# Layer 0 attention: unpadded transposes of eight heads at a time, and the second batch's keys, squares and powers half a step earlier

## The chip, the core and the metric

The kernel runs as one program on one core of a Trainium2 chip. A core has five engines that each work through their own queue of instructions in order: TensorE (PE; its weight loads are listed as PEld), VectorE (DVE), ScalarE (ACT), GpSimd (POOL) and SyncE (SP, which issues most DMAs). TensorE writes its results to PSUM, and DVE or ACT has to move them from there to SBUF, an "eviction". The metric is the device time of one execution in microseconds; the median of three runs stands for a kernel.

## The reference

The reference is four layers, each of a cross attention and a feed-forward part, over x of shape 4 x 256 x 256 and a context of 4 x 512 x 128. Only the attention of layer 0 is touched:

```python
# x: (4, 256, 256), y: the context (4, 512, 128); H = 16 heads of HD = 16, DCA = 16
def _ln(t, w, b):
    m = jnp.mean(t, axis=-1, keepdims=True)
    v = jnp.var(t, axis=-1, keepdims=True)
    return (t - m) * jax.lax.rsqrt(v + EPS) * w + b
y_dca = y[:, -DCA:, :]
y_main = y[:, :-DCA, :]
kv_dca = (y_dca @ Wkv_dca + bkv_dca).reshape(b, DCA, 2, H, HD)
k_dca = _ln(kv_dca[:, :, 0], kn_dca_w, kn_dca_b)
v_dca = kv_dca[:, :, 1]
q = _ln((x @ Wq + bq).reshape(b, s1, H, HD), qn_w, qn_b)
kv = jnp.concatenate([y_main @ Wk + bk, y_main @ Wv + bv], axis=-1)
kv = kv.reshape(b, s2, H, 2 * HD)
k = _ln(kv[..., :HD], kn_w, kn_b)
v = kv[..., HD:]
# softmax attention of q over (k, v), and another of q over (k_dca, v_dca); per head
ctx = ctx + ctx_dca
return ctx @ Wo + bo
```

What comes in is a layer norm of x, and the result is added to x. Queries and keys are normalised head by head: every group of 16 numbers gets its mean taken off and is divided by its own deviation, and then gets a weight and a bias, which are the same for all heads.

## The kernel before

**Stages.** All matrix work is in 32-bit floats. Layer 0's attention is the first stage of the program, some 150 of its 1,423 us; `bounded_path` holds it, and the order of its instructions is that of the text, on each engine. Four batches (b = 0 to 3) of 256 queries and 512 keys go through it, with two query chunks (NC) and four key chunks (NK) of 128 tokens, NQK = 6 in all. The last key chunk holds 112 ordinary keys (RD) and the 16 separate ones.

**How a batch is prepared.** `layernorm_T` transposes the normalised x, `project_q` and `project_k` compute raw queries and keys into the tile `qk` (tokens on the partitions, 16 heads x 16 numbers along a row); each returns the DVE addition that evicts it. The class `Scale` then divides by the deviation: `square` (ACT for batch 0, POOL for the others), `sum` on DVE, `power` (two small ACT instructions), `product` on DVE, which writes the tile `pad`. In `pad` each head has 32 columns, of which 16 are zeros from a memset at the start, so four heads fill 128 columns. `transposed` turns `pad` by chunks: four transposes of 128 x 128 for a chunk, into one PSUM bank `pT`, and from there an eviction to `qT` or `kT` that multiplies with the weight and adds the bias per partition (`cols`). Even chunks are evicted by ACT, odd ones by DVE; the last chunk takes two evictions, since its 16 separate keys have other weights. `norm_columns` makes `cols` at the start, by one-column matmuls from the row `rep`.

**How a batch is computed.** For each group of four heads (hg = 0 to 3) there are two half steps (kp = 0, 1), which cover two key chunks each; i = 2 hg + kp counts the eight half steps of a batch. In each, `scores` issues eight matmuls (16 passes) that contract over the 16 rows of a head, with four heads side by side at rows 0, 32, 64 and 96, into four PSUM banks `ps`, and four exponentials on ACT. `values` issues the products of the group before with the values. `quotient`, after the second half, divides on DVE. Between them, two functions issue the preparation of the next batch n = b + 1: `ahead`, between scores and values, and `between`, after the values.

| half step i | before: work for batch n |
|---|---|
| 0 | transposes of the norm (and of the context for n > 1) |
| 1 | queries |
| 2 | keys, square |
| 3 | values (n > 1), sum |
| 4 | power |
| 5 | product (ahead), the statistics of batch n + 1 (between) |
| 6 | transposes of chunks 0 to 2, tokens of batch n + 1 |
| 7 | transposes of chunks 3 to 5 (ahead) |

**What sets the order around the change.** Each engine takes its instructions in the order written. All PSUM tiles of this stage except the outputs (`o`, two banks) come from a ring of six: tile number k waits until all that read tile k - 6 are done. Four of the six are taken by each half step's scores. The tiles `qk`, `hs` (the squares) and `pad` exist once; `kT` and `qT` twice.

The lines that are used below: L1092 (memset of the pad), L1105 (memset of rep), L1175 (queries), L1191 and L1193 (keys), L1205 (values' projection), L1229 (square on POOL), L1232 (sum), L1237 and L1238 (power), L1242 to L1245 (product), L1255 (columns), L1316 (transposes), L1328 (evictions on DVE), L1330 (evictions on ACT), L1341 (scores), L1345 (exponentials), L1351 and L1360 (values), L1374 to L1382 (quotient), L918 to L921 (statistics), L926 (tokens), L938 (transposes of the norm).

Of the kernel before, what the change touches and what calls it, by code (L numbers as in the profile page):

```python
# [9 lines left out]
F32 = mybir.dt.float32  # L10
# [826 lines left out]
def bounded_path(ctx: ExitStack, tc: tile.TileContext, t, out: bass.AP, over):  # L837
# [189 lines left out]
    with tc.manual_schedule(engines={E.PE, E.Activation, E.DVE, E.Pool}):  # L1027
# [20 lines left out]
        takes = rows1[:, D:].rearrange("n (i p) -> n i p", p=P)  # L1048


        brow = w0.tile([1, 2, 2 * D], F32, tag="kT", name="brow")
        rep = w0.tile([1, 6, 4, 32], F32, tag="qT0", name="rep")
        prm = l0.tile([1, 3, 2, HD0], F32, tag="prm", name="prm")
        nc.sync.dma_start(crow[0:1, 0, :], t["L0_bq"].partition_broadcast(1))
        for i, n in enumerate(("L0_bkv", "L0_bdca")):
# [12 lines left out]
            load_x(b)  # L1068

        wo0 = l0.tile([P, 2, D], F32, tag="wo0", name="wo0")  # L1070
        wo0r = t["L0_wo"].rearrange("(q o j i x) n -> o j i x q n", q=2, o=2, j=4, i=2)
        for o in range(2):
            for j in range(4):
                r0 = 32 * j + HD0 * (1 - o)
# [13 lines left out]
        nc.gpsimd.memset(neghalf, -0.5)  # L1088


        pad = l0.tile([P, NQK * H0, 32], F32, tag="pad", name="pad")
        nc.vector.memset(pad[:, :, HD0:], 0.0)  # L1092

        nc.gpsimd.memset(takes, 1.0)
        for i, base, cm, p in (
# [70 lines left out]
        def last_context(b):  # L1166
            nc.gpsimd.tensor_copy(c_last[:, b % 2, 0, :RD], cT[:, b, SK - P : SKM])
            nc.gpsimd.tensor_copy(c_last[:, b % 2, 1, RD:], cT[:, b, SKM:])

        def project_q(b):  # L1170
            qks[b] = w0.tile([P, NQK, D], F32, tag="qk", name=f"qk{b}", bufs=1)
            pq = bank("mm", [P, NC, D], f"pq0_{b}")
            for c in range(NC):
                for d in range(ND):
                    nc.tensor.matmul(  # L1175
                        pq[:, c, :],
                        lhsT=xnTs[b][:, d, c * P : (c + 1) * P],
                        rhs=wq0[:, d, :],
                        start=(d == 0),
                        stop=(d == ND - 1),  # L1180
                    )
            return lambda: nc.vector.tensor_tensor(
                qks[b][:, :NC, :], pq, bqk[:, 0:1, :].to_broadcast([P, NC, D]), ALU.add
            )

        def project_k(b, k0):
            pk = bank("mm", [P, 2, D], f"pk{b}_{k0}")
            for k in (k0, k0 + 1):
                last = k == NK - 1
                ck = c_last[:, b % 2, 0, :] if last else cT[:, b, k * P : (k + 1) * P]  # L1190
                nc.tensor.matmul(pk[:, k - k0, :], lhsT=ck, rhs=wk0[:, 0, :], start=True, stop=not last)  # L1191
                if last:
                    nc.tensor.matmul(  # L1193
                        pk[:, k - k0, :], lhsT=c_last[:, b % 2, 1, :], rhs=wk0[:, 1, :], start=False, stop=True
                    )
            bias = bqk[:, 1:3, :] if k0 + 2 == NK else bqk[:, 1:2, :].to_broadcast([P, 2, D])
            return lambda: nc.vector.tensor_tensor(qks[b][:, NC + k0 : NC + k0 + 2, :], pk, bias, ALU.add)
# [14 lines left out]
        class Scale:  # L1212


            def __init__(self, b, a, z):
                self.n, self.name = z - a, f"{b}_{a}"
                self.src = by_head(qks[b][:, a:z])
                self.dst = pad.rearrange("p (c h) x -> p c h x", h=H0)[:, a:z, :, :HD0]
# [28 lines left out]
                )  # L1247


        cols = l0.tile([P, 3, 2], F32, tag="cols", name="cols")  # L1250

        def norm_columns():
            pn = bank("o", [P, 6], "pcols")
            for i in range(6):
                nc.tensor.matmul(  # L1255
                    pn[:, i : i + 1],
                    lhsT=rep[:, i].rearrange("o h x -> o (h x)"),
                    rhs=ident[:1, :1],
                    start=True,
                    stop=True,  # L1260
                )
            c_v = cols.rearrange("p i a -> p (i a)")
            nc.vector.tensor_scalar(c_v[:, :2], pn[:, :2], HD0 ** -0.5, None, ALU.mult)
            nc.vector.tensor_copy(c_v[:, 2:], pn[:, 2:])

        def score_bound():

# [13 lines left out]
        def bias_rows():  # L1281

            b5 = [
                brow[:, i, :].rearrange("a (q o j i x) -> a q o j i x", q=2, o=2, j=4, i=2)[:, :, :, :, 1] for i in range(2)
            ]
            for o in range(2):
                nc.vector.tensor_tensor(bval[:, :, :, 1 - o], b5[0][:, :, o], b5[1][:, :, o], ALU.add)
# [15 lines left out]

        kTs, qTs = {}, {}

        def transposed(b, chunks):

            if b not in kTs:
                kTs[b] = w0.tile([P, 4, SK], F32, tag="kT", name=f"kT{b}")
                qTs[b] = w0.tile([P, 4, S], F32, tag="qT0", name=f"qT0_{b}")  # L1310
            kT, qT = kTs[b], qTs[b]
            for c in chunks:
                pt = bank("t", [P, 4, P], f"pT{b}_{c}")
                for hg in range(4):
                    r0 = c * H0 + 4 * hg
                    nc.tensor.transpose(  # L1316
                        pt[:, hg, :], pad[:, r0 : r0 + 4, :].rearrange("p h x -> p (h x)"), ident
                    )
                if c < NC:
                    parts = [(0, qT[:, :, c * P : (c + 1) * P], pt)]  # L1320
                else:
                    k0 = (c - NC) * P
                    parts = [(1, kT[:, :, k0 : k0 + P], pt)]
                    if c == NQK - 1:
                        parts = [(1, kT[:, :, k0 : k0 + RD], pt[:, :, :RD]), (2, kT[:, :, k0 + RD :], pt[:, :, RD:])]
                for i, dst, src in parts:
                    if c % 2:
                        nc.vector.tensor_scalar(dst, src, cols[:, i, 0:1], cols[:, i, 1:2], ALU.mult, ALU.add)  # L1328
                    else:
                        nc.scalar.activation(  # L1330
                            dst, src, AF.Identity, bias=cols[:, i, 1:2], scale=cols[:, i, 0:1]
                        )

        def scores(b, hg, pT, kp):

            ps = [bank("s", [P, 2, S], f"ps0_{b}_{hg}_{kp}_{j}") for j in range(4)]
            for k in range(2):
                for j in range(4):
                    r = slice(32 * j, 32 * j + HD0)
                    k0 = (2 * kp + k) * P  # L1340
                    nc.tensor.matmul(  # L1341
                        ps[j][:, k, :], lhsT=kTs[b][r, hg, k0 : k0 + P], rhs=qTs[b][r, hg, :], start=True, stop=True
                    )
            for j in range(4):
                nc.scalar.activation(pT[kp][:, j], ps[j], AF.Exp)  # L1345
# [141 lines left out]
        warm(8)  # L1487
        xnTs[0] = layernorm_T(xn, "a0_0")
        for n in range(2):
            wv = by_head(wkv, 2 * HD0)[:, n, :, HD0:].rearrange("p (q o j) x -> p o q j x", q=2, o=2)  # L1490
# [14 lines left out]
        for add in add_k:  # L1505
            add()
        last_context(1)
        sk = Scale(0, NC, NQK)
        sq.sum()
        nc.vector.tensor_copy(  # L1510
            rep[:, :, :, :HD0],
            prm.rearrange("o i a x -> o (i a) x")[:, :, None, :].to_broadcast([1, 6, 4, HD0]),
        )
        sk.square(True)
        project_v(0)
# [4 lines left out]
        sk.power()  # L1520
        project_v(1)
        sk.product()
        transposed(0, range(NC))
        norm = Norm(1, "a0_1")
        ones_of_values()
        transposed(0, range(NC, NQK))
        first_xn = norm.tokens()


# [4 lines left out]
        def ahead(b, i):  # L1534

            n = b + 1
            if n < B:
                if i == 5:
                    scale[n].product()
                elif i == 7:  # L1540
                    transposed(n, range(3, NQK))

        def between(b, i):

            n = b + 1
            if n < B:
                if i == 0:
                    xnTs[n] = layernorm_T(xns[n], f"a0_{n}")
                    if n > 1:
                        context_T(n)  # L1550
                        last_context(n)
                elif i == 1:
                    project_q(n)()
                elif i == 2:
                    for k0 in range(0, NK, 2):
                        project_k(n, k0)()
                    scale[n] = Scale(n, 0, NQK)
                    scale[n].square(False)
                elif i == 3:
                    if n > 1:  # L1560
                        project_v(n)
                    scale[n].sum()
                elif i == 4:
                    scale[n].power()
                elif i == 5 and n + 1 < B:
                    norms[n + 1] = Norm(n + 1, f"a0_{n + 1}")
                elif i == 6:
                    transposed(n, range(3))
                    if n + 1 < B:
                        xns[n + 1] = norms[n + 1].tokens()  # L1570

# [1697 lines left out]
```

## Time and profile before

| | |
|---|---|
| median of three runs | 1415.34 us (1414.87 to 1416.9) |
| profiled execution | 1424.6 us, of which the span from first to last instruction is 1422.9 us |
| mean clock granted to TensorE over the span | 0.992 |
| attention of layer 0 (first scores to last exponentials) | 25.1 to 151.6 us |
| scores (L1341), layer 0 | 512 passes, 374 ns median of one |
| transposes of queries and keys (L1316) | 96, 273 ns median of one |
| evictions of the transposes on ACT (L1330) | 12, 789 to 799 ns |
| evictions of the transposes on DVE (L1328) | 4 of qT at 800 ns, 4 of kT at 808 ns, 4 at 741 ns and 4 small ones at 334 ns |
| product (L1245), batches 1 to 3 | 3, 1757 ns |
| square on POOL (L1229) | 3, 2748 ns |
| memset of the pad (L1092) | 1338 ns |

The durations of single PE instructions overlap: TensorE is pipelined, so what a group costs is read from the start of one group to the start of the next, not from the sum of its durations. "Idle before" is the time in which an engine had nothing it could do, and its releaser is what ended it. The profiled execution is longer than the runs' median; differences worked out in the one are taken over to the other.

### The profile page before, as it was taken

How to read it: one execution, taken by the hardware profiler on the slowest of the kernel's cores; microseconds unless marked ns; L12 is line 12 of the kernel's file. 1: busy time of each engine (PE TensorE's matmuls, PEld its weight loads, DVE VectorE, ACT ScalarE, POOL GpSimd, SP SyncE). 2: the span in 40 equal slices, each digit the busy share in tenths (PEclk: the TensorE clock that was granted, in tenths of full speed). 3: DMA queues.
4: the chain of work that ended last, by engine and by line, in shares of the span. 5: the costliest groups of instructions: out<-in, count | busy, mean ns of one | idle time of the engine just before them, and what ended most of it. 6: DMA issues, size and time to landing. Idle time of an engine off the chain costs nothing. (4 is left out here: it accounts for less than half of the span.)

```text
span 1422.9 us, 20097 instructions
## 1 busy us (share of the span) xinstructions
PE 1401.7 (99%) x7339; PEld 926.5 (65%) x7339; DVE 894.1 (63%) x2004; ACT 586.8 (41%) x1156; POOL 677.9 (48%) x809
## 2 busy tenths in 40 slices
PE   9999999999999999999999999999999999999997
PEld 7665667566566666887556666665975556666666
DVE  5657874675765557554675666558655666575675
ACT  5557464433433332255443333333544333333331
POOL 3223322576554455142576655656214765445560
PEclk9999999999999999999999999999999999999999
DMA  5000120310000000273110000000431000000000
GB/s 163 2 1 2 61 73 15 77 36 1 8 0 8 1 8 1 63 212 97 41 52 8 16 1 8 1 0 16 124 92 59 5 1 1 1 1 0 1 1 33
DMA packets 48871, 46.01 MB, mean 32 GB/s; under 512 B 8185, under 2 KB 44762, under 8 KB 48764
## 3 DMA queue, kind: packets, MB, share of 16 engines
q1 hardware_dynamic: 45308, 36.90, 8.5%
q0 software_dynamic: 2352, 6.43, 1.6%
q8 instruction: 60, 0.98, 0.3%
q10 hardware_dynamic: 1104, 1.31, 0.3%
q14 instruction: 47, 0.39, 0.1%
HBM read 38.20 MB, written 6.42 MB: 31 GB/s over the span
## 5 line engine op out<-in xcount | busy, mean ns | idle before, releaser
L1875 POOL TENSOR_TENSOR half<-pT 128x1024 f32<-128x1024 f32 x93 | 218.4, 2348 | 291.5 <-ACT pT L1859 219.7
L1856 PE MATMUL ps<-qT,cT 128*128 128x512 f32 x768 | 345.6, 593 | 0.0
L1864 PE MATMUL po<-pT,c_sb 128*128 128x512 f32 x768 | 345.3, 592 | 0.0
L1859 ACT ACTIVATE pT<-ps,mbias 128x512 f32<-128x512 f32 x384 | 264.0, 687 | 155.6 <-PE ps L1856 141.3
L1864 PEld LDWEIGHTS po<-pT,c_sb 128*128 128x128 f32 x768 | 145.8, 190 | 183.2 <-issue 183.2
L1856 PEld LDWEIGHTS ps<-qT,cT 128*128 128x128 f32 x768 | 138.9, 190 | 138.4 <-issue 136.8
L1868 ACT COPY oT<-po 128x512 f32<-128x512 f32 x96 | 56.3, 587 | 265.0 <-PE po L1864 265.0
L1911 POOL TENSOR_TENSOR oT<-oT,wide 128x512 f32<-128x512 f32 x90 | 114.5, 1292 | 17.2 <-DVE wide L1910 17.2
L1836 DVE TENSOR_TENSOR qT<-qT,paq 128x128 f32<-128x128 f32 x90 | 25.4, 282 | 95.0 <-ACT qT L1835 95.0
L1345 ACT ACTIVATE pT<-ps 128x512 f32<-128x512 f32 x128 | 65.9, 603 | 35.4 <-PE ps L1341 35.2
L1883 DVE TENSOR_TENSOR half<-half 128x512 f32<-128x512 f32 x96 | 71.4, 744 | 2.7 <-POOL half L1873 2.5
L1836 DVE TENSOR_TENSOR w<-w,pao 128x128 f32<-128x128 f32 x21 | 6.0, 286 | 106.6 <-ACT w L1835 106.6
L1885 DVE STREAM_TRANSPOSE turned<-half 128x512 f32<-128x512 f32 x96 | 68.3, 711 | 6.3
L1826 PE MATMUL paq<-xnT_a,m_sb 128*128 128x128 f32 x360 | 71.3, 280 | 0.0
L1826 PE MATMUL paq<-xx,m_x 128*128 128x128 f32 x360 | 69.6, 275 | 0.0
L1826 PEld LDWEIGHTS paq<-xnT_a,m_sb 128*128 128x128 f32 x360 | 57.3, 192 | 17.2 <-issue 8.7
L1889 DVE TENSOR_REDUCE sums<-turned 128x16 f32<-128x512 f32 x96 | 65.8, 686 | 3.3
L1826 PE MATMUL pao<-n_x,ox 128*128 128x128 f32 x336 | 65.4, 276 | 0.3 <-POOL ox L1752 0.3
L1835 ACT COPY qT<-paq 128x128 f32<-128x128 f32 x90 | 24.0, 266 | 95.4 <-PE paq L1826 95.4
L1910 DVE STREAM_TRANSPOSE wide<-rz 128x512 f32<-128x512 f32 x96 | 62.2, 685 | 0.1
L1839 DVE TENSOR_TENSOR qT<-qT,pbq 128x384 f32<-128x384 f32 x90 | 49.9, 554 | 9.4
L1826 PEld LDWEIGHTS paq<-xx,m_x 128*128 128x128 f32 x360 | 54.7, 192 | 0.0
(456 smaller groups left out, 2579.7 us busy)
## 6 DMA issues: line engine op xcount, KB each, us to landing
wq<-in_L_wqT SPq DMA_DIRECT2D x11, 512.0 KB, 5.6
wo<-in_L_wo SPq DMA_DIRECT2D x11, 512.0 KB, 6.5
yd<-yr SPq DMA_DIRECT2D x20, 128.0 KB, 4.7
w<-in_F_w SPq DMA_DIRECT2D x4, 512.0 KB, 3.4
xd<-xn_f SPq DMA_DIRECT2D x7, 256.0 KB, 2.1
wk<-in_L_wkT SPq DMA_DIRECT2D x11, 128.0 KB, 4.0
wv<-in_L_wvT SPq DMA_DIRECT2D x11, 128.0 KB, 5.2
x_sb<-in_x SPq DMA_DIRECT2D x4, 256.0 KB, 3.1
```

The source lines that it names most:

```text
L1345: nc.scalar.activation(pT[kp][:, j], ps[j], AF.Exp)
L1826: nc.tensor.matmul(p[:, at, :], lhsT=lhsT, rhs=rhs, start=(k == 0 and at == 0), stop=(k == len(of) - 1 and i == which[-1]),)
L1856: nc.tensor.matmul(ps, lhsT=cT[:, b, k * P : (k + 1) * P], rhs=qT, start=True, stop=True)
L1859: nc.scalar.activation(pT[:, k, :], ps, AF.Exp, bias=mbias[:, b, k : k + 1])
L1864: nc.tensor.matmul(po, lhsT=c_sb[:, b, k, :], rhs=pT[:, k], start=(k == 0), stop=(k == NK - 1))
L1868: done["head"] = nc.scalar.copy(raw, po).ins
L1875: nc.gpsimd.tensor_tensor(half, pT[:, 0:2], pT[:, 2:4], ALU.add)
L1883: nc.vector.tensor_tensor(part, half[:, 0], half[:, 1], ALU.add)
L1885: nc.vector.transpose(turned.rearrange("p f i -> p (f i)"), part)
L1889: nc.vector.tensor_reduce(sums[b, hp // 4][:, hp % 4, :], turned, AX.X, ALU.add)
L1910: nc.vector.transpose(wide, rzs[b, hp // 4][:, hp % 4, :, None].to_broadcast([P, NB, 32]))
L1911: eng.tensor_tensor(outs[b, hp], outs[b, hp], wide.rearrange("p f i -> p (f i)"), ALU.mult)
```

## The change

The heads are no longer padded to 32 columns. `pad` holds two groups of eight heads, 128 numbers each, per chunk, so a chunk takes two transposes instead of four, and `transposed` works on two chunks at once, with one PSUM bank. After the transpose a block of 32 rows holds two heads, an even and an odd one. For the queries the bank is evicted twice: once with weights and biases that are zero on the odd heads' rows (ACT), once with such that are zero on the even heads' rows (DVE), to different parts of `qT`. The keys are evicted once, with both heads, to `kT`, of which half is used. The scores contract over 32 rows, of which the queries make 16 zero. The first two key chunks are evicted by ACT, the last two by DVE, with a small second DVE instruction for the 16 separate keys.

`cols` has four columns pairs instead of three, and `rep` eight rows instead of six, so `norm_columns` issues eight matmuls; two small copies of POOL fill the queries' rows. The order of heads changes in the output weights' DMA, in the biases and in the copies of the values' weights. `brow`, the row of value biases, gets a buffer of its own. The memset of the pad is gone; that of `rep` covers 1,024 elements instead of 768.

For the batch n = 1 alone the order moves: its keys are projected at i = 0, ahead of the transposes of the norm, instead of i = 2; the square goes from i = 2 to 1, the sum from 3 to 2, the power from 4 to 3, the product from 5 to 4, the transposes of the first four chunks come at i = 5 and those of the last two at i = 6. For n > 1 the transposes of the first four chunks are at i = 6 and those of the last two at i = 7.

```diff
-        brow = w0.tile([1, 2, 2 * D], F32, tag="kT", name="brow")
-        rep = w0.tile([1, 6, 4, 32], F32, tag="qT0", name="rep")
+        brow = l0.tile([1, 2, 2 * D], F32, tag="brow", name="brow")
+        rep = w0.tile([1, 8, 4, 2, HD0], F32, tag="qT0", name="rep")
...
-        wo0r = t["L0_wo"].rearrange("(q o j i x) n -> o j i x q n", q=2, o=2, j=4, i=2)
+        wo0r = t["L0_wo"].rearrange("(q j o i x) n -> o j i x q n", q=2, o=2, j=4, i=2)
...
-        pad = l0.tile([P, NQK * H0, 32], F32, tag="pad", name="pad")
-        nc.vector.memset(pad[:, :, HD0:], 0.0)
+        pad = l0.tile([P, NQK, 2, P], F32, tag="pad", name="pad")
...
-            for i in range(6):
+            for i in range(8):
                 nc.tensor.matmul(
                     pn[:, i : i + 1],
-                    lhsT=rep[:, i].rearrange("o h x -> o (h x)"),
+                    lhsT=rep[:, i].rearrange("o h i x -> o (h i x)"),
...
-        def transposed(b, chunks):
+        def transposed(b, c0):
...
+            pt = bank("t", [P, 2, 2, P], f"pT{b}_{c0}")
+            for c in range(2):
+                for q in range(2):
+                    nc.tensor.transpose(pt[:, c, q, :], pad[:, c0 + c, q, :], ident)
+            if c0 < NC:
+                src = pt.rearrange("p c q t -> p q c t")
+                for o in range(2):
+                    dst = qT.rearrange("p (q o) (c t) -> p o q c t", o=2, c=2)[:, o]
+                    if o:
+                        nc.vector.tensor_scalar(dst, src, cols[:, o, 0:1], cols[:, o, 1:2], ALU.mult, ALU.add)
+                    else:
+                        nc.scalar.activation(dst, src, AF.Identity, bias=cols[:, o, 1:2], scale=cols[:, o, 0:1])
+            else:
+                k0 = (c0 - NC) * P
+                dst, src = kT[:, :, k0 : k0 + 2 * P], pt.rearrange("p c q t -> p q c t")
+                wide = dst.rearrange("p q (c t) -> p q c t", c=2)
+                if k0:
+                    nc.vector.tensor_scalar(wide, src, cols[:, 2, 0:1], cols[:, 2, 1:2], ALU.mult, ALU.add)
+                    nc.vector.tensor_scalar(
+                        wide[:, :, 1, RD:], src[:, :, 1, RD:], cols[:, 3, 0:1], cols[:, 3, 1:2], ALU.mult, ALU.add
+                    )
...
+                    nc.scalar.activation(wide, src, AF.Identity, bias=cols[:, 2, 1:2], scale=cols[:, 2, 0:1])
...
-                    r = slice(32 * j, 32 * j + HD0)
+                    r = slice(32 * j, 32 * j + 32)
                     k0 = (2 * kp + k) * P
                     nc.tensor.matmul(
-                        ps[j][:, k, :], lhsT=kTs[b][r, hg, k0 : k0 + P], rhs=qTs[b][r, hg, :], start=True, stop=True
+                        ps[j][:, k, :], lhsT=kTs[b][r, hg // 2, k0 : k0 + P], rhs=qTs[b][r, hg, :], start=True, stop=True
                     )
...
+        for o in range(2):
+            nc.gpsimd.tensor_copy(rep[:, 2 * o : 2 * o + 2, :, o, :], prm[:, 0, :, None, :].to_broadcast([1, 2, 4, HD0]))
...
-        transposed(0, range(NC))
+        transposed(0, 0)
         norm = Norm(1, "a0_1")
         ones_of_values()
-        transposed(0, range(NC, NQK))
+        transposed(0, 2)
+        transposed(0, 4)
...
-                if i == 5:
+                if i == (4 if n == 1 else 5):
                     scale[n].product()
-                elif i == 7:
-                    transposed(n, range(3, NQK))
+                elif i == 7 and n > 1:
+                    transposed(n, 4)
...
                 if i == 0:
+                    if n == 1:
+                        for k0 in range(0, NK, 2):
+                            project_k(n, k0)()
                     xnTs[n] = layernorm_T(xns[n], f"a0_{n}")
...
-                elif i == 2:
+                elif i == 2 and n > 1:
                     for k0 in range(0, NK, 2):
                         project_k(n, k0)()
+                elif i == 3 and n > 1:
+                    project_v(n)
+                if i == (1 if n == 1 else 2):
                     scale[n] = Scale(n, 0, NQK)
                     scale[n].square(False)
...
+                elif i == (2 if n == 1 else 3):
                     scale[n].sum()
-                elif i == 4:
+                elif i == (3 if n == 1 else 4):
                     scale[n].power()
-                elif i == 5 and n + 1 < B:
+                if i == 5 and n + 1 < B:
                     norms[n + 1] = Norm(n + 1, f"a0_{n + 1}")
-                elif i == 6:
-                    transposed(n, range(3))
+                if i == (5 if n == 1 else 6):
+                    transposed(n, 0)
+                    transposed(n, 2)
+                if i == 6:
+                    if n == 1:
+                        transposed(n, 4)
                     if n + 1 < B:
                         xns[n + 1] = norms[n + 1].tokens()
```

More of the change, by code (lines that the diff above doesn't have):

```diff
@@ L1168, in last_context, with raw_heads @@
             nc.gpsimd.tensor_copy(c_last[:, b % 2, 1, RD:], cT[:, b, SKM:])
+        def raw_heads(b):
+            if b not in qks:
+                qks[b] = w0.tile([P, NQK, D], F32, tag="qk", name=f"qk{b}", bufs=1)
         def project_q(b):
-            qks[b] = w0.tile([P, NQK, D], F32, tag="qk", name=f"qk{b}", bufs=1)
+            raw_heads(b)
             pq = bank("mm", [P, NC, D], f"pq0_{b}")
@@ L1186, in project_k @@
         def project_k(b, k0):
+            raw_heads(b)
             pk = bank("mm", [P, 2, D], f"pk{b}_{k0}")
@@ L1217, in __init__ @@
                 self.src = by_head(qks[b][:, a:z])
-                self.dst = pad.rearrange("p (c h) x -> p c h x", h=H0)[:, a:z, :, :HD0]
+                self.dst = pad.rearrange("p c q (h x) -> p c (q h) x", x=HD0)[:, a:z]
                 self.sq = w0.tile([P, NQK, H0, HD0], F32, tag="hs", name=f"hs{self.name}", bufs=1)[:, a:z]
@@ L1247, in product @@
                 )
-        cols = l0.tile([P, 3, 2], F32, tag="cols", name="cols")
+        cols = l0.tile([P, 4, 2], F32, tag="cols", name="cols")
         def norm_columns():
-            pn = bank("o", [P, 6], "pcols")
-            for i in range(6):
+            pn = bank("o", [P, 8], "pcols")
+            for i in range(8):
                 nc.tensor.matmul(
                     pn[:, i : i + 1],
-                    lhsT=rep[:, i].rearrange("o h x -> o (h x)"),
+                    lhsT=rep[:, i].rearrange("o h i x -> o (h i x)"),
                     rhs=ident[:1, :1],
@@ L1262, in norm_columns @@
             c_v = cols.rearrange("p i a -> p (i a)")
-            nc.vector.tensor_scalar(c_v[:, :2], pn[:, :2], HD0 ** -0.5, None, ALU.mult)
-            nc.vector.tensor_copy(c_v[:, 2:], pn[:, 2:])
+            nc.vector.tensor_scalar(c_v[:, :4], pn[:, :4], HD0 ** -0.5, None, ALU.mult)
+            nc.vector.tensor_copy(c_v[:, 4:], pn[:, 4:])
         def score_bound():
@@ L1283, in bias_rows @@
             b5 = [
-                brow[:, i, :].rearrange("a (q o j i x) -> a q o j i x", q=2, o=2, j=4, i=2)[:, :, :, :, 1] for i in range(2)
+                brow[:, i, :].rearrange("a (q j o i x) -> a q o j i x", q=2, o=2, j=4, i=2)[:, :, :, :, 1] for i in range(2)
             ]
@@ L1304, in bounded_path @@
         kTs, qTs = {}, {}
-        def transposed(b, chunks):
+        def transposed(b, c0):
             if b not in kTs:
-                kTs[b] = w0.tile([P, 4, SK], F32, tag="kT", name=f"kT{b}")
+                kTs[b] = w0.tile([P, 4, SK], F32, tag="kT", name=f"kT{b}")[:, :2]
                 qTs[b] = w0.tile([P, 4, S], F32, tag="qT0", name=f"qT0_{b}")
             kT, qT = kTs[b], qTs[b]
[L1312 to L1317, printed above, removed]
-                    )
-                if c < NC:
-                    parts = [(0, qT[:, :, c * P : (c + 1) * P], pt)]
-                else:
[L1322 to L1332, printed above, removed]
@@ L1489, in bounded_path @@
         for n in range(2):
-            wv = by_head(wkv, 2 * HD0)[:, n, :, HD0:].rearrange("p (q o j) x -> p o q j x", q=2, o=2)
+            wv = by_head(wkv, 2 * HD0)[:, n, :, HD0:].rearrange("p (q j o) x -> p o q j x", q=2, o=2)
             for o in range(2):
@@ L1509, in bounded_path @@
         sq.sum()
+        for o in range(2):
+            nc.gpsimd.tensor_copy(rep[:, 2 * o : 2 * o + 2, :, o, :], prm[:, 0, :, None, :].to_broadcast([1, 2, 4, HD0]))
         nc.vector.tensor_copy(
-            rep[:, :, :, :HD0],
-            prm.rearrange("o i a x -> o (i a) x")[:, :, None, :].to_broadcast([1, 6, 4, HD0]),
+            rep[:, 4:].rearrange("o i h a x -> o i (h a) x"),
+            prm[:, 1:].rearrange("o i a x -> o (i a) x")[:, :, None, :].to_broadcast([1, 4, 8, HD0]),
         )
@@ L1553, in between @@
                     project_q(n)()
-                elif i == 2:
+                elif i == 2 and n > 1:
                     for k0 in range(0, NK, 2):
                         project_k(n, k0)()
+                elif i == 3 and n > 1:
+                    project_v(n)
+                if i == (1 if n == 1 else 2):
                     scale[n] = Scale(n, 0, NQK)
                     scale[n].square(False)
-                elif i == 3:
-                    if n > 1:
-                        project_v(n)
+                elif i == (2 if n == 1 else 3):
                     scale[n].sum()
-                elif i == 4:
+                elif i == (3 if n == 1 else 4):
                     scale[n].power()
-                elif i == 5 and n + 1 < B:
+                if i == 5 and n + 1 < B:
                     norms[n + 1] = Norm(n + 1, f"a0_{n + 1}")
-                elif i == 6:
-                    transposed(n, range(3))
+                if i == (5 if n == 1 else 6):
[4 more added lines that the diff above has]
+                        transposed(n, 4)
                     if n + 1 < B:
```

## The prediction

> **What bounds the kernel now.** I read the page's busy rows first, then the busy time by stage, then the order of time inside layer 0. The page's first row already says where to look:
>
> ```profile
> PE 1401.7 (99%) x7339; PEld 926.5 (65%) x7339; DVE 894.1 (63%) x2004; ACT 586.8 (41%) x1156; POOL 677.9 (48%) x809
> ```
>
> TensorE is nearly never without work. The chain that ended last lies in the final layers and says nothing of layer 0, so layer 0 has to be read from its own stretch (columns: window, length, then busy time and count of PE, PEld, DVE, ACT and POOL, granted clock, DMA share, GB/s):
>
> ```profile
> 20.00:50.00 30.00, 27.98 (x291) 18.80 (x289) 19.75 (x41) 20.77 (x44) 9.54 (x22) 1.00 0.17 56
> 50.00:80.00 30.00, 29.10 (x320) 19.18 (x324) 18.40 (x32) 18.24 (x40) 6.88 (x9) 0.94 0.01 1
> 80.00:110.00 30.00, 28.67 (x267) 18.69 (x260) 16.40 (x33) 15.88 (x31) 8.93 (x11) 0.89 0.01 2
> 110.00:140.00 30.00, 30.00 (x366) 18.22 (x366) 24.12 (x56) 22.50 (x46) 8.09 (x11) 1.00 0.01 2
> ```
>
> PE bounds all four stretches; DVE and ACT have a quarter or more free, but over a step or two either can hold PE up. The clock is below 1 in two stretches. Their cause, second by second:
>
> ```profile
> 49.00:50.00 1.00, 0.13 (x4) 0.00 (x0) 0.93 (x3) 0.83 (x2) 0.92 (x2) 1.00 0.00 0
> 50.00:51.00 1.00, 0.10 (x1) 0.10 (x2) 0.90 (x3) 1.00 (x3) 0.81 (x2) 1.00 0.00 0
> 52.00:53.00 1.00, 1.00 (x6) 1.00 (x5) 0.61 (x1) 0.35 (x1) 0.00 (x0) 0.50 0.00 0
> 91.00:92.00 1.00, 1.00 (x16) 0.20 (x4) 0.00 (x0) 0.00 (x0) 0.00 (x0) 0.50 0.00 0
> ```
>
> PE stood still at 49 to 51, and then ran at half clock. The timeline names the wait (start, length, engine, line, operation; in brackets the idle time and its releaser):
>
> ```profile
> 46.46 1.29 PEld L1316 LDWEIGHTS pT<-ident,pad 128*128 128x128 f32 x12 [0.41 <-ACT pT L1345]
> 47.92 0.81 PEld L1341 LDWEIGHTS ps<-qT,kT 16*128 16x128 f32 x16 [0.17 <-issue]
> 50.04 0.80 DVE L1328 TENSOR_SCALAR qT<-pT,cols 128x512 f32<-128x512 f32 x1
> 50.90 2.57 PE L1316 MATMUL pT<-ident,pad 128*128 128x128 f32 x12 [1.77 <-DVE qT L1328]
> ...
> 85.03 1.80 PE L1341 MATMUL ps<-qT,kT 16*128 16x256 f32 x10 [1.33 <-DVE qT L1328]
> 86.76 2.82 PE L1316 MATMUL pT<-ident,pad 128*128 128x128 f32 x12
> ...
> 119.08 0.80 DVE L1328 TENSOR_SCALAR qT<-pT,cols 128x512 f32<-128x512 f32 x1
> ```
>
> All of PE's PSUM tiles but the outputs share a ring of six banks. A transpose's bank comes free when its eviction has run, and DVE's eviction of the queries stands behind the product, a quotient and the next batch's statistics. For batches 1 and 2 (the second and third) PE waits for it; for batch 3, which has no statistics, it doesn't.
>
> **Transposes.** Each batch needs 12 instead of 24. Twelve took 47.92 - 46.46 = 1.46 us, 0.122 us each, so 48 fewer are 5.8 us of PE work. The Trainium skill (TensorE: Matmul & The Clock Gate, Part 1) gives about 56 ns for a warm 128-column matmul, by which it would be 2.7 us; this trace has twice that, and I take the trace. What survives of it goes by batch.
>
> *Batch 3.* Eight transposes stay ahead of the last scores of batch 2, four come after. The last of the scores' four banks now falls on the queries' bank, which DVE frees at 119.88; PE got to that matmul at about 120.0. So of the 4 x 0.122 = 0.49 saved ahead of it only 0.1 counts, and 8 x 0.122 = 0.98 after it. **1.1 us.**
>
> *Batch 2.* DVE is the pacer: product from 77.55, quotient, statistics, then the queries at 84.18 to 84.98. None of that changes, so the 0.49 us saved ahead of the stall only lengthens it (1.33 to 1.8 us). After it, eight transposes fewer at the half-clock rate of 2.82/12 = 0.235 are 1.9 us, and the 0.65 us that the second group waited for banks goes: 2.5 us. But the clock stays at half until about 92.1, so half of these 2.5 us is given back to the work that moves into the half-clock stretch. **1.3 us**, 0.8 to 3.2: the upper end if the clock recovers a window sooner.
>
> *Batch 0 (start).* Here DVE and ACT pace. The columns now take 16 passes instead of the 12 of this row:
>
> ```profile
> 18.03 1.49 PE L1255 MATMUL pcols<-ident,rep 1*128 1x1 f32 x12
> ```
>
> that is 0.5 us more, and DVE waits for them before its two products: the keys' product ends at 23.6 instead of 23.11. After it come four transposes (0.5), 0.16 of latency and one eviction on ACT (0.79): the first scores can start at 25.2, whole. Before, they started at 25.12 but waited for DVE's third eviction at 25.8. Then:
>
> ```profile
> 29.29 1.59 PEld L1175 LDWEIGHTS pq<-wq,xnT_a 128*128 128x128 f32 x8 [0.33 <-ACT xnT_a L941]
> 33.29 1.16 PEld L1191 LDWEIGHTS pk<-wk,cT 128*128 128x128 f32 x6 [0.41 <-ACT pT L1345]
> ```
>
> The keys' projection (33.29 to 35.65, 2.36 us) moves ahead of the norm's transposes, where PE waited for DVE (0.84) and then for ACT (0.33). Walked on: scores 1.1 to 26.3, keys to 28.7, norm's transposes 0.7 to 29.4 (their input is ready at 27.6), scores to 30.5, queries. Before, the same work came to 29.29 + 2.36 = 31.65. **1.2 us**, 0.3 to 1.8.
>
> *Batch 1.* The square on POOL (2.75 us, after its vector memsets, which end near 30) starts after the queries' add, at 33 instead of 36.6. DVE's sum then stands ahead of the first quotient instead of behind it. From the end of the square, near 36, DVE has sum 2.0, quotient 2.5, product 2.6: the product ends near 43.2, while PE reaches the transposes near 42.2: a new wait of about 1 us. On go quotient 2.5, statistics 1.7, the queries' eviction 0.8: 48.2. PE, through the eight transposes, scores and values, comes to the last four near 46.4, and their bank is the one that DVE's queries hold: 1.8 us again. ACT's powers ahead of the exponentials cost PE another 0.5. Against these 3.3 us stand, before, the scores from 43.01, which took 2.45 us to the values at 45.46 instead of 1.07, and the 1.77: 3.2 us. The stall is moved, not removed. Twelve transposes, 1.5 us, less 0.1: **1.4 us**, 0.5 to 2.2.
>
> **The clock.** The Trainium skill (same page, HAM oscillation) warns of PE-idle gaps over about 3.4 us. By that rule neither kernel's stalls would touch the clock, and none of the half-clock time would be there. The trace has stalls of 1.77 and 1.33 us each followed by half clock, for about 3.5 and 6.8 us, which lost half of that, 5.1 us. I go by the trace: a stall of 1.8 us in batch 1 and one of 1.8 in batch 2 will be punished alike, so nothing is got back there. One window of 3.4 us more or less is 1.7 us; that widens the range both ways.
>
> **At nothing.** The pad's memset (1.34 us of DVE) goes, the other one grows by a third (0.70 to about 0.93): DVE then waits for x anyway (0.67 idle at 3.98). One eviction on ACT (0.79) and one on DVE (0.81) a batch go; on ACT it is cover, on DVE it lies after the read that decides. Two small copies on POOL, at most 0.3 us each, run under the values' projection, which ends at 18.1. The output weights' eight DMAs take other rows in pieces of the same size, at 10 to 15 us in SP's queue, ahead of nothing that waits. The biases' own buffer changes no queue. The new waits of the queries' second eviction (on ACT's first one) lie under the product or the statistics.
>
> **Sum:** 1.2 + 1.4 + 1.3 + 1.1 = 5.0 us; with some hope for an earlier recovery of the clock, 5.3. The profiled execution of 1424.6 us (span 1422.9) would come to 1419.3; the runs' median stands 9.3 lower, at 1415.34, and comes to **1410.0 us**.
>
> **Rivals.**
> - *The stalls dissolve (chance 0.17).* Batch 1 keeps its clock and batch 2 recovers after one window: 5.0 + 1.7 + 1.7 = 8.4 us, 1406.9. For it: the second batch's stall is split in two, and a gate that looks at windows may see neither. Against: the longer part is as long as today's.
> - *The gain is lost in waits (0.13).* PE walks into DVE's chain in batch 1 for as long as it saved, and a half-clock window comes on top: 5.0 - 1.4 - 1.7 = 1.9 us, 1413.4, no change that can be told. For it: DVE is at 0.9 and more in each second from 44 to 52.
> - *Scores over 32 rows are dearer (0.05), slower.* They now contract over 32 rows, half of them zeros, in 512 passes. These take 1.07 us for 16 here (67 ns each):
>
> ```profile
> 35.65 0.74 PEld L1341 LDWEIGHTS ps<-qT,kT 16*128 16x128 f32 x16 [0.33 <-issue]
> 36.72 0.59 PEld L1351 LDWEIGHTS po<-pT,vals 128*32 128x32 f32 x16 [0.33 <-issue]
> ```
>
> At 10 ns more per pass the gain is gone; at 25 ns more it is 12.8 - 5.0 = 7.8 us slower, 1423.1. Bounds: below zero there is no reason; above, 240 ns per pass as in the queries' projection, if the four quarters no longer ran side by side. Against: the values beside it read 128 rows at the same 1.0 us for 16, and the slices of 32 rows still don't overlap. I take zero.
> - *The change doesn't do what it says:* the order of instructions on each engine shows it does, so this has no share.
>
> **Numbers.** The forecast has 0.65, the rivals 0.17, 0.13 and 0.05. Half of 0.2 is cut off at each end: 1405.8 to 1413.2. A measurement of this kernel tells 0.2%, 2.8 us, from no change: below 1412.5 is faster. Of the forecast's own 0.65 about 0.04 lies above that. Faster 0.78, same 0.16, slower 0.06.
>
> **What would show it.** In the profile after: 48 transposes instead of 96; scores from about 25.2; the queries' projection of batch 1 near 30.5; a wait of PE for DVE's queries in batch 1 near 46 to 48 and in batch 2 near 80, each followed by half clock; the end of the attention some 5 us earlier. Wrong would be: score groups longer than 1.07 us, a stall of batch 1 over 3 us, or a clock of 1.00 throughout.

## The result and the profile after

The changed kernel takes 1409.33 us (median of six runs, 1407.28 to 1410.79); the kernel before, timed beside it, takes 1416.93 (1414.87 to 1422.92). The ratio is 0.9937, with a 95% interval of 0.9916 to 0.9958: faster by some 6 to 12 us. The profiled execution has a span of 1405.6 us, 17.3 less than before, which is more than the runs show: the profiled execution of before, 1424.6 us, is longer than each of its six runs, that of the changed kernel, 1407.28, is the shortest of its six. The experiments say where the difference lies.

The page's busy row and the busy time by stage, in the columns of before:

```profile
PE 1386.9 (99%) x7295; PEld 915.2 (65%) x7295; DVE 890.8 (63%) x1999; ACT 583.7 (42%) x1152; POOL 677.9 (48%) x811
```

```profile
20.00:50.00 30.00, 27.07 (x304) 17.70 (x302) 22.46 (x46) 21.36 (x45) 10.26 (x23) 1.00 0.22 76
50.00:80.00 30.00, 29.30 (x330) 19.02 (x323) 19.92 (x36) 20.56 (x45) 8.21 (x10) 1.00 0.01 2
80.00:110.00 30.00, 30.00 (x343) 19.10 (x343) 19.15 (x33) 19.53 (x42) 8.51 (x11) 1.00 0.00 1
```

PE is still the bound, and the clock is now 1.00 where it was 0.94 and 0.89. The waits have not all gone, though (timeline of the changed kernel; start, length, engine, line, operation, in brackets idle time and releaser):

```profile
29.79 1.99 PE L1178 MATMUL pq<-wq,xnT_a 128*128 128x256 f32 x8
...
42.99 1.06 PE L1319 MATMUL pT<-ident,pad 128*128 128x128 f32 x8 [1.33 <-DVE pad L1249]
...
46.06 0.66 PE L1319 MATMUL pT<-ident,pad 128*128 128x128 f32 x4
46.85 0.80 DVE L1325 TENSOR_SCALAR qT<-pT,cols 128x512 f32<-128x512 f32 x1
47.71 1.13 PE L1347 MATMUL ps<-qT,kT 32*128 32x256 f32 x12 [0.36 <-DVE qT L1325]
...
77.36 1.77 PE L1347 MATMUL ps<-qT,kT 32*128 32x256 f32 x16
78.97 0.80 DVE L1325 TENSOR_SCALAR qT<-pT,cols 128x512 f32<-128x512 f32 x1
79.83 0.65 PE L1319 MATMUL pT<-ident,pad 128*128 128x128 f32 x4 [0.70 <-DVE qT L1325]
```

In batch 1 PE waits 1.33 us for the product, as forecast, but then hardly for the queries: its last four transposes start at 46.06 without waiting for the eviction of 46.85 to 47.65, and the scores behind them wait 0.36. In batch 2 all 16 passes of the last scores run at 77.36, ahead of the queries' eviction; only the four transposes behind them wait, 0.70 us, and by then the exponentials have their input.

**By stage.** The table gives for every profile the time from the first scores of one batch to those of the next (batch 3: to the last values), which the clock and the waits can be read from. "Behind" is what is left of the span after the start of the last values. The preparation of batch n runs in the row of batch n - 1: the forecast's terms for the start and for batch 1 are in the row of batch 0, its batch 2 in that of batch 1, its batch 3 in that of batch 2.

| profile | batch 0 | batch 1 | batch 2 | batch 3 | sum | behind |
|---|---|---|---|---|---|---|
| before | 30.29 | 37.88 | 31.66 | 26.07 | 125.9 | 1271.9 |
| after | 25.35 | 32.70 | 30.65 | 26.07 | 114.8 | 1266.0 |
| e1, unpadded, old order | 25.87 | 32.72 | 30.65 | 26.06 | 115.3 | 1268.3 |
| e2, padded, new order | 26.86 | 34.64 | 31.65 | 26.07 | 119.2 | 1269.4 |
| e3, padded, statistics later | 27.37 | 34.35 | 31.99 | 26.07 | 119.8 | 1266.9 |
| e4, padded, scores over 32 rows | 30.28 | 34.64 | 31.65 | 26.07 | 122.6 | 1265.6 |
| e5, unpadded, old order, statistics later | 25.68 | 33.74 | 30.98 | 26.07 | 116.5 | 1265.9 |
| e6, transposes and statistics late | 23.37 | 31.94 | 30.64 | 26.07 | 112.0 | 1266.5 |
| e7, after with 2 us more on DVE | 25.35 | 36.03 | 30.65 | 26.07 | 118.1 | 1267.2 |
| e8, after again | 25.35 | 32.71 | 30.64 | 26.08 | 114.8 | 1265.6 |
| e9, before again | 30.15 | 34.64 | 31.65 | 26.08 | 122.5 | 1267.2 |
| e10, before again | 31.92 | 36.19 | 31.66 | 26.07 | 125.8 | 1266.8 |

"Behind" is work that the change doesn't touch, and it spreads over 6 us by itself; the first profile of before had the longest one. Part of that is the clock: behind the attention, leaving out the last 5 us of the span, the first profile of before has 10.2 us at half clock (from 590 and from 751 us), that of the changed kernel 3.4 (from 580). If half of such time is lost, an estimate, that makes 3.4 us of the difference of 5.9. So of the 17.3 us between the two spans 5.9 are behind the attention, and are not evidence for the change; 11.1 are the attention's, and 0.3 lie ahead of the first scores.

### The profile page after: what moved, and what is told of

It reads as the page before. It is cut to its first block, busy times and chain, and to the rows that moved or that the text cites. A ratio compares the mean times of both kernels' runs of the same rounds, so it can differ in the third digit from the quotient of the medians.

```text
span 1405.6 us, 19998 instructions
## 1 busy us (share of the span) xinstructions
PE 1386.9 (99%) x7295; PEld 915.2 (65%) x7295; DVE 890.8 (63%) x1999; ACT 583.7 (42%) x1152; POOL 677.9 (48%) x811
## 4 chain that ended last, share of the span: by engine, by line
PE 91%; DVE 4%; POOL 3%; issue 2%; ACT 0%; DMA 0%; DVEq 0%; POOLq 0%; ACTq 0%
PE ps L1873 23%; PE po L1881 22%; PE paq L1843 6%; PE pao L1843 5%; PE pbq L1843 4%; PE pbo L1843 4%; PE ps L1347 2%; PE paf L1431 2%; PE pyf L1481 2%; PE pgu L2396 2%; PE po L1357 2%; PE psh L2218 1%; PE py L1963 1%; PE pn L1002 1%; PE pb L2723 1%
## 5 line engine op out<-in xcount | busy, mean ns | idle before, releaser
L1928 POOL TENSOR_TENSOR oT<-oT,wide 128x512 f32<-128x512 f32 x90 | 114.4, 1290 | 17.3 <-DVE wide L1927 17.3
```

Source lines behind the costliest of these rows:

```text
L1928: eng.tensor_tensor(outs[b, hp], outs[b, hp], wide.rearrange("p f i -> p (f i)"), ALU.mult)
```

## The experiments

**Each half of the change alone.** e1 has the new layout, with batch 1 in the old order:

```diff
-                if i == (4 if n == 1 else 5):
+                if i == 5:
                     scale[n].product()
-                elif i == 7 and n > 1:
+                elif i == 7:
                     transposed(n, 4)
...
-                if i == (5 if n == 1 else 6):
+                if i == 6:
                     transposed(n, 0)
                     transposed(n, 2)
```

with keys, square, sum and power back at 2, 2, 3 and 4 in the same way.

> Unpadded transposes as in the changed kernel, but batch 1 prepared in the old order (keys at half step 2, transposes at 6 and 7). Theory (two parts of about equal worth: fewer transposes with the queries' bank no longer in the last scores' way, and the earlier order of batch 1): batches 2 and 3 as in the changed kernel (first scores of batch 2 some 31.4 us after those of batch 1 + 1.4, no half clock there), batch 1 later by the 1.2 us of the keys that no longer fill the wait for the norm: 2 to 4 us faster than before, 2 to 4 slower than the changed kernel. Rival (the order of batch 1 is what mattered): batch 1 stalls for the queries' eviction as before with half clock after it, and the kernel is within 1.5 us of before.

Measured: ratio 0.9929 (0.9911 to 0.9947) to before, median 1406.93 us. It is no slower than the changed kernel (0.9937), not 2 to 4 us slower. Both parts of the expectation that told of batch 1 fell: PE does wait 1.4 us for the norm's tokens, which the early keys filled, but the stall for the queries is gone in the old order too, with the unpadded transposes alone, and batch 0 is only 0.5 us longer than in the changed kernel.

e2 has the old layout with the new order:

```diff
-                elif i == 6:
-                    transposed(n, range(3))
+                if i == (5 if n == 1 else 6):
+                    transposed(n, range(4 if n == 1 else 3))
+                if i == 6:
+                    if n == 1:
+                        transposed(n, range(4, NQK))
```

> Padded transposes as before, with batch 1 prepared in the new order (four chunks at half step 5, two at 6). Theory: only the 1.2 us of the filled wait at the start is gained in batch 1, its stall is moved, and batch 2 stalls 1.3 us and runs at half clock as before: 0.5 to 2.5 us faster than before. Rival (the order is what mattered): 4 us or more faster.

Measured: ratio 0.9968 (0.9949 to 0.9986), median 1411.88 us, some 4.5 us faster, which is in the rival's range, though the interval (2 to 7 us) reaches into the theory's. Its waits of PE between 20 and 150 us (who waited for whom: total, times, longest), and those of e1:

```profile
PE pT L1321 <- DVE pad L1250: 1.3, 1, 1.3
PE ps L1346 <- DVE qT L1333: 1.3, 1, 1.3
...
PE pT L1321 <- DVE qT L1333: 0.2, 1, 0.2
```

```profile
PE pxn_a L938 <- DVE xn_a L926: 1.4, 1, 1.4
PE pT L1319 <- DVE pad L1249: 0.8, 1, 0.8
PE pT L1319 <- DVE qT L1325: 0.7, 1, 0.7
```

The first 1.3 of e2 is batch 1's product, the 0.2 what is left of batch 1's wait for the queries, the other 1.3 that of batch 2, which the order of batch 1 doesn't touch; the half clock that the theory expected behind it did not come (1.00 in all of layer 0, batch 1 at 34.64 us). So each half alone takes the queries' wait of batch 1 away. In the row of batch 0 e1 gains 4.4 us on the first profile of before, e2 3.4, and both together 4.9, of which 1.7 are that profile's half clock: the halves overlap in what they take away, and the earlier order is worth 0.5 us on top of the transposes, which the runs can't tell from nothing.

**The wait alone.** e3 is the kernel before with the statistics moved behind the evictions:

```diff
-                elif i == 5 and n + 1 < B:
-                    norms[n + 1] = Norm(n + 1, f"a0_{n + 1}")
                 elif i == 6:
                     transposed(n, range(3))
                     if n + 1 < B:
-                        xns[n + 1] = norms[n + 1].tokens()
+                        norms[n + 1] = Norm(n + 1, f"a0_{n + 1}")
+                elif i == 7 and n + 1 < B:
+                    xns[n + 1] = norms[n + 1].tokens()
```

> The kernel before, with nothing changed but the place of the next batch's norm statistics on DVE: behind the evictions of half step 6 instead of ahead of them (its tokens go to step 7). Takes away the wait of PE for DVE's eviction of the queries in batches 1 and 2, but no transposes. Theory (the stalls bring the half clock): the queries are evicted 1.7 us earlier, both stalls fall below 0.5 us, the clock in layer 0 stays at 1.00, and the kernel is 4 to 8 us faster than before, with as many transposes. Rival (the clock drops for another reason): the stalls go, the clock still drops, 1 to 3 us faster.

Measured: ratio 0.998 (0.9969 to 0.9991), median 1413.61: 1.3 to 4.4 us faster, less than the theory's 4 to 8. The theory's mechanism is there, and not the rival's lower clock: the queries are evicted at 48.04, ahead of the statistics, and the clock is 1.00 in all of layer 0.

```profile
48.04 0.80 DVE L1328 TENSOR_SCALAR qT<-pT,cols 128x512 f32<-128x512 f32 x1
48.76 0.42 DVE L918 BATCH_NORM_STATS2 st_a<-x_sb 128x6 f32<-128x256 f32 x1
48.89 0.42 PEld L1316 LDWEIGHTS pT<-ident,pad 128*128 128x128 f32 x4 [0.49 <-DVE qT L1328]
...
55.34 0.41 PE L938 MATMUL pxn_a<-ident,xn_a 128*128 128x128 f32 x2 [1.01 <-DVE xn_a L926]
```

The last row shows what took part of it back: the tokens come late, and the next batch's norm waits for them, 1.9 us in all, against 0.4 before. A further part is that before does not lose to the clock in every execution what it lost in the first profile, as e4, e9 and e10 show below.

**Rows of the scores.** e4 changes one line of before, `slice(32 * j, 32 * j + HD0)` to `slice(32 * j, 32 * j + 32)`.

> The kernel before, with the scores contracting over 32 rows instead of 16 (the added rows are the zeros of the padding). Theory: 16 passes still take 1.07 us, no change, within 1 us of before. Rival (wider rows are dearer): more than 1.07 us per 16 passes, 5 us slower at 10 ns a pass.

```profile
35.55 0.74 PEld L1341 LDWEIGHTS ps<-qT,kT 32*128 32x128 f32 x16 [0.33 <-issue]
36.63 0.59 PEld L1351 LDWEIGHTS po<-pT,vals 128*32 128x32 f32 x16 [0.33 <-issue]
```

Ratio 0.9997 (0.9987 to 1.0007), and 1.08 us from the one group to the next: 32 rows cost what 16 did. This profile shows something else. It has the same two waits as before, but batch 1 takes 34.64 us instead of 37.88:

```profile
84.94 1.13 PE L1341 MATMUL ps<-qT,kT 32*128 32x256 f32 x10 [1.33 <-DVE qT L1328]
85.99 1.53 PE L1316 MATMUL pT<-ident,pad 128*128 128x128 f32 x12
```

The same 1.33 us of waiting, and the 12 transposes take 1.53 us instead of 2.82: the clock stayed up.

**Transposes alone.** e5 is e1 with the statistics moved as in e3.

> Unpadded transposes, batch 1 in the old order, norm statistics behind the evictions of half step 6 (and tokens at step 7), as in the padded kernel with the statistics moved. The two differ only in the transposes, and neither stalls for the queries. Theory (what the 48 fewer transposes are worth by themselves is their count by 0.122 us, less a few tenths where batch 0 is paced by DVE): the last values of the attention start at 138.5 to 140 us of the span, 4.5 to 6 earlier than the padded one's 144.6. Rival (part of the gain of the change is only the stalls): less than 3 us earlier.

Measured from the first scores, e5 takes 116.5 us and e3 119.8: 3.3 less, between the theory's and the rival's ranges. PE waits 3.4 us for tokens in e5 and 1.9 in e3 (first e5, then e3):

```profile
PE pxn_a L938 <- DVE xn_a L926: 3.4, 4, 1.5
PE pxn_a L938 <- DVE xn_a L926: 1.9, 4, 1.0
```

PE comes to the norm's transposes earlier, and the tokens don't come earlier by as much. With these 1.5 us added the 48 transposes come to 4.8 of the 5.8 us that their count gave; with all waits of PE between 20 and 150 us (4.8 us in e5, 2.6 in e3) they come to 5.5. The ratio is 0.9949 (0.9936 to 0.9961).

**Wait and clock.** e7 puts DVE work ahead of the queries' eviction in batch 2 of the changed kernel; the sums are not used.

```diff
                     norms[n + 1] = Norm(n + 1, f"a0_{n + 1}")
+                    if n == 2:
+                        for _ in range(3):
+                            dm = small.tile([P, NC], F32, tag="dm", name=f"dm{_}")
+                            nc.vector.tensor_reduce(dm, x_sb[3], AX.X, ALU.add)
```

> The changed kernel with three sums over x (0.7 us each, results unused) on DVE ahead of the eviction of the queries of batch 2. Theory (a long wait of PE brings the half clock): PE waits 0.7 + 2.1 = 2.8 us near 80 us, half clock follows for one or two windows of 3.4 us, and the start of batch 2 is 2.1 + 1.7 to 3.4 us later. Rival (the clock drops for something else, and the wait only costs itself): 2.1 us later and clock 1.00.

```profile
79.02 1.86 DVE L1583 TENSOR_REDUCE dm<-x_sb 128x2 f32<-128x512 f32 x3
80.80 0.80 DVE L1325 TENSOR_SCALAR qT<-pT,cols 128x512 f32<-128x512 f32 x1
...
81.65 1.11 PE L1319 MATMUL pT<-ident,pad 128*128 128x128 f32 x4 [2.48 <-DVE qT L1325]
82.69 1.94 PE L1357 MATMUL po<-pT,vals 128*32 128x256 f32 x16
```

Microsecond by microsecond (window, length, busy time and count of PE, PEld, DVE, ACT and POOL, granted clock, DMA share, GB/s):

```profile
81.00:82.00 1.00, 0.35 (x2) 0.35 (x3) 1.00 (x3) 0.00 (x0) 0.00 (x0) 0.77 0.00 0
82.00:83.00 1.00, 1.00 (x8) 0.56 (x10) 0.77 (x3) 0.00 (x0) 0.35 (x1) 0.50 0.00 0
...
85.00:86.00 1.00, 1.00 (x12) 0.68 (x4) 0.64 (x1) 0.00 (x0) 0.00 (x0) 1.00 0.00 0
```

The wait grew by 1.78 us (0.70 to 2.48), and batch 1 by 3.33 (32.70 to 36.03). What is over, 1.55, is about half of the one stretch at half clock, 3.4 us from 81.5 to 85. The median is 1411.99, ratio 0.9971 (0.9955 to 0.9986) to before. In this one profile the longer wait brought the half clock, where the 0.70 us of the changed kernel had not in two; it cost itself and 1.5 us more.

**Both kernels profiled again.**

> The changed kernel once more, beside the others on the same chip. Theory: its layer 0 is free of half clock in this profile too (waits of at most 1.3 us), the last values start within 0.5 us of 139.6, and the median is within 2 us of 1409.3. Rival (that the clock stayed up was luck): half clock in layer 0 in this profile, 1.7 us or more later.

> The kernel before, looked at once more. Theory (a wait of PE brings half clock only if it falls so in the chip's own windows): the same waits for the queries, 1.8 and 1.3 us, in batches 1 and 2, and each followed by half clock in some executions only: batch 0 takes 28.6 us (no half clock) or 30.3, batch 1 34.6 or 36 to 38. Rival (the waits always bring it): 30.3 and 37.9 as in the first profile.

> As the look before it: the same waits, half clock after each in some executions only.

The changed kernel repeats its stages to 0.01 us, with no half clock in layer 0; its first scores come 0.5 us later in the span, and so do its last values, at 140.2 (median 1408.70, ratio 0.9949, interval 0.9932 to 0.9966). The kernel before doesn't. These are 80 to 110 us of e9, then 20 to 50 and 80 to 110 us of e10:

```profile
80.00:110.00 30.00, 28.67 (x308) 19.06 (x308) 18.32 (x34) 18.39 (x40) 9.64 (x12) 1.00 0.01 2
20.00:50.00 30.00, 28.53 (x286) 18.78 (x284) 18.25 (x37) 19.53 (x41) 8.98 (x22) 0.94 0.21 72
80.00:110.00 30.00, 28.68 (x292) 19.11 (x284) 18.10 (x34) 17.11 (x36) 9.25 (x12) 0.94 0.01 2
```

Its wait of 1.8 us was followed by 3.4 us of half clock in all four profiles that have it (before, e4, e9, e10). Its wait of 1.3 us was followed by 6.8 us of half clock in the first, by 3.4 in e10, and by none in e4 and e9. e10 has one more stretch of 3.4 us in batch 0, from 28.5 us, and the only waits of PE ahead of it since 20 us are of 0.50 and 0.43 us, which the other three profiles have too, without half clock there. So a wait for the queries is not the only thing that brings it. The wait of 1.8 us did as e9's rival says, that of 1.3 as its theory. The four attentions are 125.9, 122.6, 122.5 and 125.8 us long, 124.2 in the mean, against 114.8 of the changed kernel.

**A version without the waits.** e6 keeps the early keys, square, sum, power and product, and puts batch 1's transposes where the other batches have theirs, the statistics behind them and the tokens ahead of the last quotient:

```diff
-                elif i == 7 and n > 1:
+                elif i == 7:
                     transposed(n, 4)
+                    if n + 1 < B:
+                        xns[n + 1] = norms[n + 1].tokens()
...
-                if i == 5 and n + 1 < B:
-                    norms[n + 1] = Norm(n + 1, f"a0_{n + 1}")
-                if i == (5 if n == 1 else 6):
+                if i == 6:
                     transposed(n, 0)
                     transposed(n, 2)
                 if i == 6:
-                    if n == 1:
-                        transposed(n, 4)
                     if n + 1 < B:
-                        xns[n + 1] = norms[n + 1].tokens()
+                        norms[n + 1] = Norm(n + 1, f"a0_{n + 1}")
```

> The changed kernel with the transposes of batch 1 at half steps 6 and 7 as in the other batches (its keys, square, sum, power and product stay early), the statistics behind the evictions of half step 6 and the tokens ahead of the last quotient. Theory: the 1.3 us that PE waits for the product in batch 1, the 0.4 for the queries there and the 0.7 in batch 2 all go, 1.5 to 2.5 us in the span's first 140 us, clock 1.00 throughout layer 0, a median 1 to 3 us below the changed kernel's 1409.3. Rival: the tokens then come too late for the next batch's transposes and take it back, within 1 us of the changed kernel.

```profile
43.99 1.09 PE L1319 MATMUL pT<-ident,pad 128*128 128x128 f32 x8
45.01 1.31 PE L1347 MATMUL ps<-qT,kT 32*128 32x256 f32 x16
46.52 0.66 PE L1319 MATMUL pT<-ident,pad 128*128 128x128 f32 x4 [0.21 <-ACT kT L1338]
```

The waits for the product in batch 1 and for the queries are gone, and the attention takes 112.0 us, 2.8 less than the changed kernel's, a little over what the theory gave, so the rival's loss to late tokens did not come. The median is 1407.93 us (1402.0 to 1410.31), ratio 0.9939 (0.992 to 0.9959): it beats the kernel before, but the runs can't tell it from the changed kernel, whose two medians are 1409.33 and 1408.70.

## Why the prediction was right, and where it was not

The time, 1409.33, lies within 1 us of the forecast of 1410.0, and the sign was right; that it is so close is in part luck. Two things cancel in it: the gain was larger than forecast (7.6 us by the two medians, against 5.3), and the median of before was 1.6 us higher with more runs than the three it was worked from. The attention ended 11.4 us earlier in the profile, not some 5, and one of the forecast's own signs of being wrong came, a clock of 1.00 (in all of layer 0). The saved work was forecast rightly; the stalls and the clock behind them were not.

- *Transposes.* 96 fell to 48. The 0.122 us each was about right: in batch 2 of the table, where nothing else changes, 12 fewer are worth 1.01 us, as against the 1.1 forecast for batch 3, and e5 against e3 leaves 4.8 of 5.8 once the tokens are counted. The 56 ns of the Trainium skill (TensorE: Matmul & The Clock Gate, Part 1), which the page has for bf16 operands, would have made it 2.7. The guess that those ahead of a fixed wait are lost fits it too.
- *Start.* Right in its steps, a little low in size. The columns took 1.94 us instead of 1.49, and the scores started at 24.85, whole (forecast 25.2). The queries' projection of batch 1 came at 29.79 instead of 30.5, so this stretch gave 31.65 - 29.79 = 1.9 us instead of 1.2. The 0.84 us that the forecast took for PE's wait ahead of the norm's transposes is that of the weight load; PE itself stood 0.44. In e1, where nothing fills it, that wait grew to 1.44.
- *Batch 1.* The wait for the product was forecast at about 1 us and came, 1.33. The second one, "1.8 us again", failed: it was 0.36. The step behind it was that the last four transposes would take the bank that DVE's query eviction holds. They did not wait; the wait for that eviction came at the third bank of the scores behind them, so that seems to be the one that took it. By count, the transposes are the sixth tile after the queries' bank, and the tile that waited is the ninth. Nor was the stall only moved, as the prediction put it. In all, the first scores of batch 1 came 5.2 us earlier in the span (50.20 instead of 55.41); without the 1.9 of the start and the 1.7 of before's half clock, 1.6 are left, against a forecast of 1.4, so that here only the make-up of the sum was wrong.
- *Batch 2.* The same step failed: "the last of the scores' four banks now falls on the queries' bank". That bank is the sixth tile after the queries'; the whole group ran ahead of the eviction, and the wait was 0.70 behind it, at the seventh tile, instead of 1.8 inside it. In the kernel before, both waits do fall on the sixth tile. Why they don't in the changed kernel stays open: the profile names no banks. At full clock the batch gained 34.64 - 32.70 = 1.9 us (e9's row against the changed kernel's), forecast 1.3; by the first profile it gained 5.2, the rest of which is the clock. The 0.65 us that "the second group waited for banks" was a misreading: it stands beside a weight load, and PE was at work on the scores.
- *The clock.* That is where the forecast case was wrong and the first rival right in the profile. "A stall of 1.8 us in batch 1 and one of 1.8 in batch 2 will be punished alike" holds of a stall of that length (four times in four, and 2.48 in e7), but neither came. In both profiles of the changed kernel the clock stays at 1.00 through layer 0. What was not seen is that before's loss of 5.1 us was one draw: the same waits cost it about 1.7 us of clock in two of the other three profiles and some 3.4 in the third, which lost another 1.7 elsewhere. The rival's number, 1406.9, is further from the time than the forecast's. Its own ground, one wait split in two, is not what did it: both waits shrank, by the places at which they came, because the held bank was asked for later.
- *The dearer scores* fell with e4 (1.08 us for 16 passes against 1.07), *the gain lost in waits* with the table.
- *At nothing.* The pad's memset, the small copies and the moved DMAs leave no wait of PE behind them in the profile; the columns' first weight load waited 0.33 us for the two copies (0.71 us together), under the values' projection. The first scores came earlier, not later.

How much of the median's 7.6 us is work and waits, and how much clock, can be bounded, not split exactly. With 1.7 us taken off batch 0 for its one half-clock stretch, before's attention at full clock is 28.6 + 34.6 + 31.7 + 26.1 = 121.0 us, 6.2 more than 114.8; the clock then costs before some 1.5 to 5 us in a given execution, by its four profiles. What the rest of the spread behind the attention comes from was not tried.

## What to carry to other kernels

When PSUM banks go round a shared ring, an eviction that frees a bank late stalls whoever takes that bank next, so ask for each bank what is queued ahead of its last reader, and put work that nobody awaits (here, statistics) behind it. But don't rely on counted positions to find who takes it: read it from the waits in the profile, since here the wait came one and three tiles later than counted, and was 0.70 and 0.36 us instead of 1.8. And take a profile twice before a loss to the clock is put into a sum: it may be there in one execution and not in the next.

## What the runs showed of the hardware

A wait of PE of 1.77 or 1.78 us was followed by half clock in four of four profiles (before, e4, e9, e10), one of 2.48 in e7's, and the 1.33 us of batch 2 in two of four. The other waits of that size were not: two of 1.33 us in e2, that for the product in batch 1 of the changed kernel (also 1.33) in its two profiles and in e7, 1.44 in e1, and 1.43 and 1.54 in e5. All of these are far below the length that the Trainium skill warns of (TensorE: Matmul & The Clock Gate, HAM oscillation: over some 3.4 us), so by the measurement that length is too lax.

The same page (Part 1) has the gate look at free-running windows of 3.4 us. The runs agree with that much: the stretches of half clock in layer 0 are 3.4 us long (81.5 to 85 in e7) or twice that, and within a profile they start whole multiples of 3.41 us apart (in e10 at 28.49, 52.38 and 86.52 us: 7 and 10 of them). And an equal wait in an equal program is punished in one execution and not in the other. So waits of 1.3 to 1.5 us are at the edge, with half clock behind two of twelve. What decides there stays open, and so does what brought the stretch at 28.49 us in e10.
